# Recurrent block, sparse feed-forward and attention on one core: the last block's norms and sparse inputs on VectorE

## The chip, the cores and the metric

The kernel runs on one core of a Trainium2 chip. A core has a matrix engine (TensorE, PE in the profile), a vector engine (VectorE, DVE), a scalar engine (ScalarE, ACT), a general engine (GpSimd, POOL), and queues for transfers, most of which are issued by SyncE (SP). Each engine takes its own instructions in the order in which they were compiled and waits at semaphores for the others. The metric is the device time of one execution in microseconds (us); the shown time is the median of several runs.

## The reference, cut to what matters

The input is x, 4 x 1024 tokens of 256 features. Four residual layers follow one another, each on the layer-normalized x: a linear recurrent unit, a sparse feed-forward layer, attention with 8 heads, and the sparse feed-forward layer once more. What the change touches is the end of the first and the start of the second:

```python
out = out2[0] - out2[1] + o
y = jax.nn.gelu(out @ w1_w + w1_b, approximate=False)
y = y @ w2_w + w2_b + out
y = (y - mean) * rsqrt(var + LN_EPS) * ln_g + ln_b          # x = x + y
...
xc = jnp.einsum('ngf,gf->ng', x2d.reshape(n, g, 4), conv_w) + conv_b
xn = (xc - mean(xc)) * rsqrt(var(xc) + BN_EPS) * gamma + beta # over all 4096 tokens
logits = gelu(xn) @ lin_w.T + lin_b                          # once for outputs, once for inputs
score_out = softmax(logits)
s_v_out, s_i_out = top_k(score_out, 32)
full = x @ weight              # only its 32 best of 256 outputs are kept, times their scores
in_branch = x_sparse @ weight  # x with only its 32 best of 256 inputs, times their scores
x = x + out_branch + in_branch + bias
```

Two points set the order. The second norm in the sparse layer is a batch norm: its mean and variance are taken over all tokens, so no GELU of that layer can start before the last token's convolution. And the convolution wants the layer norm of the finished x of the last tokens.

## The kernel before

Tokens lie on the 128 partitions, so 4096 tokens are 32 tiles, and four tiles make a block; there are 8 blocks, 0 to 7 (NBLK = 8), and the last is block 7. x stays in SBUF throughout. A scheduler fixes the order of instructions on each engine at compile time; `tc.issue_after(i)` is a demand on it that what follows is issued after instruction i. It is the compiled order that the chip executes.

**Recurrent layer** (`Lru`, up to about 265 us). `outputs` makes out for one block, then GELU, the second product and the residual `ot` (VectorE, L455), turns it back into `py` (TensorE, L465), takes the layer norm of `py` with bn_stats and bn_aggr (`layer_norm`, tiles `ly_*`; the inverse root is a chain of small VectorE steps, L55 to L66, then the shift, minus mean times rstd, L136), and adds y to x. For the last block this is cut in two halves of 256 tokens (`halves`), whose buffers are given as `bufs`. There the normalized `yn` is made by ScalarE (L474) and multiplied by the gain and added to x by VectorE (L479, L480). The base is added to x on GpSimd beforehand.

**Start of the sparse layer** (`Ffn.head`, first called for earlier blocks in between). For a block it takes the layer norm of x (tiles `fx_*`, result `norm_f`), makes `xn` per tile (ScalarE, L145, in `normalized_t`), transposes it (TensorE, L147, into `pt`), copies `pt` to `ft` (ScalarE, L524), writes `ft` to DRAM as `tt` (SP, L527), convolves it (TensorE, L529, into `pc`), adds the bias (ScalarE, L533, `xc`) and takes bn_stats of it (VectorE, L534). `xn` has two buffers. Block 6 goes through `head` as a whole in two pairs of tiles, block 7 as two calls of one pair. So the end of the recurrent layer has four rounds of pt, ft, pc: two for block 6 and two for block 7.

**Batch norm and first tiles.** `norm_scale` makes the scale `bs` and the shift `bt` of the batch norm on VectorE (L542 to L548, with the small steps at L55 to L66). `gelu(0)` and `gelu(1)` (ScalarE, L587) treat the 512 tokens of blocks 0 and 1. `Ffn.tile` makes the logits of a tile `pl` (TensorE, L554 and L556), the first maxima (VectorE, L674), the negated maximum `nm` (GpSimd, L613), the exponentials `ex` (ScalarE, L615), the remaining steps of the top 32 (match_replace and max on VectorE, L674), the reciprocal `rs` (VectorE, L630), the dense product `pf` from `tt` (TensorE, L567), and the two branches (`ob`, `xg`, and the additions to x at L659 and L662). The first eight tiles run so before attention starts; the other 24 run inside the attention phase as side work.

**Weights for later.** `wfs` is the sparse weight in two parts, a rounded high part (ScalarE, L1151) and the remaining low part (GpSimd, L1152); it is first used in the attention phase. `attn_weights` loads the attention weights (SP: `wa` at L712, `wdf` at L715), splits `wdf` in `wd` (L718, L719), squares it (`wds`, GpSimd, L724) and goes on to make products of the attention weights in between the first tiles. On SP stand in this order: the last writes of `ft`, the first `tt` load, the `wa` loads, `wdf`, the second `tt` load.

**Attention and the last layer.** The keys of batch 0 need the finished x of tiles 0 to 7 (layer norm `ax_*`, transposes at L147, products `pml`, then the two parts `kh` and `kl`), and its first scores `sc` follow. Attention runs head by head, 345 to 1285 us, with the other sparse tiles merged in; the last sparse layer follows to the end.

Of the kernel before, what the change touches and what calls it, by code (L numbers as in the profile page):

```python
# [10 lines left out]
F32 = mybir.dt.float32  # L11
# [4 lines left out]
AF = mybir.ActivationFunctionType  # L16
ALU = mybir.AluOpType
# [4 lines left out]
P = 128  # L22
# [6 lines left out]
NBLK = B * T // 512  # L29
# [15 lines left out]
V_BETA = 22  # L45
# [75 lines left out]
    return c, s, last  # L121


def layer_norm(nc, pool, tag, views, rstd=None, shift=None):

    n = len(views)
    mv = pool.tile([P, n, 2], F32, tag=f"{tag}_mv", name=f"{tag}_mv")
    if rstd is None:
        both = pool.tile([P, 2, n], F32, tag=f"{tag}_rs", name=f"{tag}_rs")
        rstd, shift = both[:, 0, :], both[:, 1, :]  # L130
    for i, v in enumerate(views):
        st = pool.tile([P, 6], F32, tag=f"{tag}_st", name=f"{tag}_st", bufs=4)
        nc.vector.bn_stats(st, v)
        nc.vector.bn_aggr(mv[:, i, :], st)
    rsqrt(nc, pool, tag, mv[:, :, 1], rstd)
    nc.vector.scalar_tensor_tensor(shift, mv[:, :, 0], -1.0, rstd, ALU.mult, ALU.mult)  # L136
    return rstd, shift


def normalized_t(nc, pool, psum, tag, ptag, views, rstd, shift, ident):  # L140

    pt = psum.tile([P, KD, len(views) * P], ptag, "pt")
    for i in range(len(views)):
        xn = pool.tile([P, D], F32, tag="fx_xn", name="xn", bufs=2)
        nc.scalar.activation(xn, views[i], AF.Identity, bias=shift[:, i : i + 1], scale=rstd[:, i : i + 1])  # L145
        for k in range(KD):
            nc.tensor.transpose(pt[:, k, i * P : (i + 1) * P], xn[:, k * P : (k + 1) * P], ident)  # L147
    return pt
# [46 lines left out]
class Lru:  # L195
# [226 lines left out]
    def outputs(self, r, xs, xnt, h, pairs, last, tag="po", bufs=None):  # L422

        nc, w, sp, vecs = self.nc, self.w, self.sp, self.vecs
        tiles = range(2 * pairs[0], 2 * pairs[-1] + 2)
        sl = slice(tiles[0] * P, (tiles[-1] + 1) * P)
        n = len(tiles) * P
        ot, zt = bufs or self.buffers()
        for c in range(KD):
            co = slice(c * P, (c + 1) * P)  # L430
            po = self.psum.tile([P, 512], tag, "po")[:, 0:n]
            self.inputs(po, r, 2, c, xnt, sl, stop=False)
            terms = [
                (self.w_mid[r][k][e][:, co], h[k][e][:, sl.start + r : sl.stop + r]) for k in range(KD) for e in range(2)
            ]
            for i, (lt, v) in enumerate(terms):
                nc.tensor.matmul(po, lt, v, start=False, stop=(i == len(terms) - 1))
            nc.scalar.activation(ot[:, c, :], po, AF.Identity, bias=self.ob[:, r, c : c + 1])
            yield
        for c in range(KD):  # L440
            pz = self.psum.tile([P, 512], "pu", "pz")[:, 0:n]
            for k in range(KD):
                nc.tensor.matmul(
                    pz, w[:, k, 2, c * P : (c + 1) * P], ot[:, k, :], start=(k == 0), stop=(k == KD - 1)
                )
            last_gelu = nc.scalar.activation(zt[:, c, :], pz, AF.Gelu, bias=vecs[:, V_B1 + c : V_B1 + c + 1])
        self.last_gelu = last_gelu.ins
        yield
        for c in range(KD):
            pz = self.psum.tile([P, 512], tag, "pz2")[:, 0:n]  # L450
            for k in range(KD):
                nc.tensor.matmul(
                    pz, w[:, k, 3, c * P : (c + 1) * P], zt[:, k, :], start=(k == 0), stop=(k == KD - 1)
                )
            nc.vector.scalar_tensor_tensor(  # L455
                ot[:, c, :], pz, vecs[:, V_B2 + c : V_B2 + c + 1], ot[:, c, :], ALU.add, ALU.add
            )
        yield
        pys = []
        for j in range(len(tiles) // 2):  # L460
            py = self.psum.tile([P, 2, D], "pu" if tag == "pu" else "py", "py")
            for i in range(2):
                tk = slice((2 * j + i) * P, (2 * j + i + 1) * P)
                for k in range(KD):
                    nc.tensor.transpose(py[:, i, k * P : (k + 1) * P], ot[:, k, tk], self.ident)  # L465
            pys += [py[:, 0, :], py[:, 1, :]]
        rstd, shift = layer_norm(nc, sp, f"ly{len(tiles)}", pys)
        gain, base = self.brow[:, 0, :], self.brow[:, 1, :]
        for q, tile_q in enumerate(tiles):
            xt = xs[tile_q]  # L470
            yn = sp.tile([P, D], F32, tag="yn", name="yn", bufs=3)
            if last:
                nc.gpsimd.tensor_tensor(xt, xt, base, ALU.add)
            self.last_yn = nc.scalar.activation(  # L474
                yn, pys[q], AF.Identity, bias=shift[:, q : q + 1], scale=rstd[:, q : q + 1]
            ).ins
            if last:
                engine = nc.vector if bufs else nc.gpsimd
                engine.tensor_tensor(yn, yn, gain, ALU.mult)  # L479
                engine.tensor_tensor(xt, xt, yn, ALU.add)  # L480
            else:
                nc.gpsimd.tensor_tensor(yn, yn, gain, ALU.mult)
                nc.gpsimd.tensor_tensor(yn, yn, base, ALU.add)
                nc.gpsimd.tensor_tensor(xt, xt, yn, ALU.add)
        yield


class Ffn:
# [9 lines left out]
        self.counted = 0  # L498
        self.dram, self.turned, self.full = None, {}, {}

    def head(self, blk, sp, psum, ptag, pairs=(0, 1), xtag="fx", ttag="ft"):


        nc, w = self.nc, self.w
# [3 lines left out]
        norm = self.norm[blk]  # L508
        tiles = slice(2 * pairs[0], 2 * pairs[-1] + 2)
        tokens = slice(256 * pairs[0], 256 * pairs[-1] + 256)  # L510
# [8 lines left out]
        for i, j in enumerate(pairs):  # L519
            r = slice(2 * j, 2 * j + 2)  # L520
            xs = self.x[blk * 4 + 2 * j : blk * 4 + 2 * j + 2]
            pt = normalized_t(nc, sp, psum, xtag, ptag, xs, norm[:, 0, r], norm[:, 1, r], w.ident)
            tt = sp.tile([P, KD, 256], F32, tag=ttag, name="ft", bufs=2 if self.dram else 1)
            nc.scalar.copy(tt, pt)  # L524
            yield
            if self.dram:
                nc.sync.dma_start(self.turned[blk][:, :, j * 256 : (j + 1) * 256], tt)  # L527
            for k in range(KD):
                nc.tensor.matmul(  # L529
                    pc[k * 64 : (k + 1) * 64, i * 256 : (i + 1) * 256], w.cw[:, k, :], tt[:, k, :], start=True, stop=True  # L530
                )
# [6 lines left out]
    def norm_scale(self, sp):  # L538

        nc, w = self.nc, self.w  # L540
        bmv = sp.tile([P, 2], F32, tag="bmv", name="bmv")
        nc.vector.bn_aggr(bmv, self.bst[:, 0 : self.counted, :].rearrange("p a b -> p (a b)"))  # L542
        bs = self.bp.tile([P, 1], F32, tag="bs", name="bs", bufs=2)
        rsqrt(nc, sp, "bn", bmv[:, 1:2], bs)
        nc.vector.tensor_tensor(bs, bs, w.vecs[:, V_GAMMA : V_GAMMA + 1], ALU.mult)
        bt = self.bp.tile([P, 1], F32, tag="bt", name="bt", bufs=2)
        nc.vector.tensor_tensor(bt, bmv[:, 0:1], bs, ALU.mult)
        nc.vector.tensor_tensor(bt, w.vecs[:, V_BETA : V_BETA + 1], bt, ALU.subtract)  # L548
        self.bs, self.bt = bs, bt

    def logits_product(self, dst, i):
        nc, w = self.nc, self.w
# [29 lines left out]
            nc.sync.dma_start(self.full[blk][:, 2 * j : 2 * j + 2, :], v)  # L582
            yield

    def gelu(self, blk):
        x = self.xc[blk]
        return self.nc.scalar.activation(x, x, AF.Gelu, bias=self.bt, scale=self.bs).ins  # L587

    def tile(self, i, sp, psum, tags, out=None, fast=False, parts=None, tt=None, fine=False):
# [395 lines left out]
def run(*gens):  # L985
    for g in gens:
        for _ in g:
            pass
# [58 lines left out]
def tile_kernel(ctx: ExitStack, tc: tile.TileContext, x_in, w_lru, vecs_in, rows, w_ffn, lin_t, w_attn, w_down, out):  # L1047
    nc = tc.nc
# [7 lines left out]
    x = [t[:, q, :] for t in blocks for q in range(4)]  # L1056
# [12 lines left out]
    w = Weights()  # L1069
# [12 lines left out]
    with ExitStack() as c1:  # L1082
# [56 lines left out]
        for i in (0, 1, 0, 1, 0, 1, 1):  # L1139
            next(halves[i])  # L1140
        with tc.issue_after(lru.last_gelu):
            run(f1.head(NBLK - 2, lru.sp, psum, "pt"))
        run(*(f1.head(NBLK - 1, lru.sp, psum, "pu", (i,), "lx", "zt") for i in range(2)))

    with ExitStack() as c2:
        sp = c2.enter_context(tc.tile_pool(name="at_s", bufs=2))
# [2 lines left out]
        wqk, wvo, wd = two([P, KD, HEADS * HD], "wqk"), two([P, PAIRS, D], "wvo"), two([P, KD, P], "wd")  # L1149
        wfs = two([P, KD, D], "wf")  # L1150
        nc.scalar.copy(wfs[0], w.wf)  # L1151
        nc.gpsimd.tensor_tensor(wfs[1], w.wf, wfs[0].bitcast(F32), ALU.subtract)  # L1152
        at = Attention(tc, x, ident, ident64, wqk, wvo, wd, sp, wp)
        with ExitStack() as c4:
            psum = Banks(
# [1 line left out]
            )  # L1157
            fp = c4.enter_context(tc.tile_pool(name="f_t", bufs=4))
            weights = attn_weights(nc, fp, psum, "at", w_attn, w_down, wqk, wvo, wd, at, ident64)
            f1.norm_scale(sp)  # L1160
            tts = [f1.load(blk, fp, f"tt{blk}") for blk in range(2)]
            f1.gelu(0)
            with tc.issue_after(f1.gelu(1)):
                warm(nc, sp, AF.Exp)
            tiles = [
# [174 lines left out]
```

## Time and profile before

| | |
|---|---|
| time, median of 3 runs | 1511.01 us (1509.11 to 1512.66) |
| the profiled execution's own time | 1507.37 us |
| its span in the trace | 1505.6 us |
| busy, TensorE (PE) | 1278.4 us, 85% |
| busy, VectorE (DVE) | 1181.0 us, 78% |
| busy, ScalarE (ACT) | 1018.0 us, 68% |
| busy, GpSimd (POOL) | 683.0 us, 45% |
| mean granted TensorE clock | 0.952 of full speed |
| instructions in the trace | 28728 |

In a row of the timeline the first number is the start in us from the start of the span, the second the time that this group of instructions took; then come the engine, the line of the kernel, the operation, its output and inputs by name, their sizes and types, and how many there are (x2: two such instructions grouped). In square brackets stands how long the engine was idle before it, and what ended that idle time. PEld is the loading of weights into TensorE, SPq a transfer issued by SP. The TensorE clock is the share of full speed that was granted.

### The profile page before, as it was taken

How to read it: one execution, taken by the hardware profiler on the slowest of the kernel's cores; microseconds unless marked ns; L12 is line 12 of the kernel's file. 1: busy time of each engine (PE TensorE's matmuls, PEld its weight loads, DVE VectorE, ACT ScalarE, POOL GpSimd, SP SyncE). 2: the span in 40 equal slices, each digit the busy share in tenths (PEclk: the TensorE clock that was granted, in tenths of full speed). 3: DMA queues.
4: the chain of work that ended last, by engine and by line, in shares of the span. 5: the costliest groups of instructions: out<-in, count | busy, mean ns of one | idle time of the engine just before them, and what ended most of it. 6: DMA issues, size and time to landing. Idle time of an engine off the chain costs nothing. (4 is left out here: it accounts for less than half of the span.)

```text
span 1505.6 us, 28728 instructions
## 1 busy us (share of the span) xinstructions
PE 1278.4 (85%) x10136; PEld 947.3 (63%) x10136; DVE 1181.0 (78%) x3682; ACT 1018.0 (68%) x2152; POOL 683.0 (45%) x849
## 2 busy tenths in 40 slices
PE   4899998887998998898988988889999999576765
PEld 3645555465776777676766766677777877244544
DVE  8988676796778876977777778777676675599998
ACT  5334535666878877787877687877877776566664
POOL 2024523352555454454534543545443534067776
PEclk9999999799999999999999999999999999678898
DMA  3010000432553443353434344433444444000000
GB/s 119 20 55 15 22 21 29 144 105 50 92 88 72 81 86 67 61 89 75 77 73 79 61 69 80 75 74 71 71 85 85 85 85 85 1 15 25 22 25 29
DMA packets 288754, 96.52 MB, mean 64 GB/s; under 512 B 268377, under 2 KB 284770, under 8 KB 288610
## 3 DMA queue, kind: packets, MB, share of 16 engines
q1 hardware_dynamic: 283522, 88.90, 29.6%
q10 hardware_dynamic: 5088, 5.78, 1.1%
q8 instruction: 80, 1.31, 0.4%
q14 instruction: 64, 0.52, 0.1%
HBM read 16.01 MB, written 11.53 MB: 18 GB/s over the span
## 5 line engine op out<-in xcount | busy, mean ns | idle before, releaser
L898 POOL TENSOR_TENSOR pd<-pr,pd 128x1024 f16<-128x1024 f32 x128 | 273.6, 2142 | 259.3 <-ACT pd L897 200.1
L890 DVE TENSOR_REDUCE nm<-sc 128x1 f32<-128x1024 f32 x256 | 308.4, 1217 | 74.8 <-PE sc L886 73.2
L894 ACT ACTIVATE pr<-sc,nm 128x1024 f32<-128x1024 f32 x256 | 286.1, 1120 | 89.8 <-DVE nm L892 54.7
L886 PE MATMUL sc<-kh,qs 128*128 128x512 f32 x512 | 184.4, 438 | 28.5 <-ACT pr L894 21.0
L886 PE MATMUL sc<-kl,qs 128*128 128x512 f32 x512 | 161.7, 396 | 0.0
L674 DVE MATCH_REPLACE8 wk<-m,wk 128x256 f32<-128x256 f32 x384 | 155.3, 408 | 0.1
L910 ACT COPY p<-ptp 128x512 f32<-128x512 f32 x224 | 124.1, 591 | 44.4 <-PE ptp L905 32.5
L674 DVE MAX8 m<-wk 128x8 f32<-128x256 f32 x384 | 150.7, 413 | 0.4
L905 PE MATMUL ptp<-ident,pr 128*128 128x128 f32 x1024 | 139.2, 276 | 13.3 <-ACT pr L894 12.0
L930 PE MATMUL pmo<-p,la 128*64 128x128 f32 x2048 | 140.2, 284 | 5.9 <-ACT ft L524 2.9
L905 PEld LDWEIGHTS ptp<-ident,pr 128*128 128x128 f32 x1024 | 116.2, 141 | 35.5 <-ACT pr L894 21.7
L897 ACT CAST pd<-pr 128x1024 f16<-128x1024 f32 x128 | 133.5, 1054 | 4.6 <-DMA d<-pd 3.6
L930 PEld LDWEIGHTS pmo<-p,la 128*64 128x64 f32 x2048 | 119.6, 142 | 24.7 <-issue 4.7
L886 PEld LDWEIGHTS sc<-kh,qs 128*128 128x128 f32 x512 | 85.2, 195 | 53.9 <-ACT pr L894 32.9
L886 PEld LDWEIGHTS sc<-kl,qs 128*128 128x128 f32 x512 | 96.6, 189 | 23.2 <-issue 1.4
L930 PE MATMUL pmo<-d,lb 128*64 128x128 f16 x3072 | 101.5, 220 | 8.7 <-DVE qs L853 2.6
L930 PEld LDWEIGHTS <-lb 128*64 128x64 f16 x3072 | 90.7, 110 | 26.6 <-issue 19.9
L628 POOL TENSOR_TENSOR ex<-ex,wk 128x512 f32<-128x512 f32 x61 | 77.8, 1276 | 58.4 <-DVE wk L674 48.9
L926 POOL COPY rows<-rs 128x128 f32<-128x128 f32 x128 | 36.3, 297 | 120.4 <-PE pmo L938 71.7
L941 DVE TENSOR_TENSOR on<-pmo,rb 128x128 f32<-128x128 f32 x128 | 36.4, 284 | 64.8 <-ACT rb L940 64.3
L147 PE MATMUL pt<-ident,xn 128*128 128x128 f32 x256 | 48.9, 310 | 44.0 <-ACT xn L145 32.3
L699 PE MATMUL pf<-wf,vt 128*128 128x256 f32 x288 | 80.9, 424 | 3.9 <-ACT vt L697 3.4
(307 smaller groups left out, 2766.1 us busy)
## 6 DMA issues: line engine op xcount, KB each, us to landing
tt<-ft SPq DMA_DIRECT2D x16, 256.0 KB
tt<-tt SPq DMA_DIRECT2D x8, 512.0 KB
out<-x SPq DMA_DIRECT2D x32, 128.0 KB
x<-in_x ACTq DMA_DIRECT2D x6, 512.0 KB
pf<-pfs SPq DMA_DIRECT2D x12, 256.0 KB
full<-pf SPq DMA_DIRECT2D x24, 128.0 KB
d<-pd SPq DMA_TRANSPOSE x128
wa<-in_w_attn SPq DMA_DIRECT2D x2, 640.0 KB
```

The lines of the kernel that those rows point to most:

```text
L147: nc.tensor.transpose(pt[:, k, i * P : (i + 1) * P], xn[:, k * P : (k + 1) * P], ident)
L628: pool.tensor_tensor(ex, ex, wk, ALU.subtract)
L674: ins = make(*args).ins
L699: nc.tensor.matmul(dst, vt[:, k, :], w.wf[:, k, :], start=(k == 0 and bias is None), stop=(k == KD - 1))
L886: nc.tensor.matmul(sc[:, sl], qs[:, j, q * P : (q + 1) * P], kk[:, sl], start=(i == 0), stop=(i == 1))
L890: nc.vector.tensor_reduce(nm, sc, AX.X, ALU.max, negate=True)
L894: nc.scalar.activation(pr, sc, AF.Exp, bias=nm, accum_out=ssum[:, j : j + 1])
L897: nc.scalar.copy(pd[:, 0, :], pr)
L898: nc.gpsimd.tensor_tensor(pd[:, 1, :], pr, pd[:, 0, :], ALU.subtract)
L905: nc.tensor.transpose(pt[:, kk, :], pr[:, kc * P : (kc + 1) * P], self.ident)
L910: nc.scalar.copy(dst, pt)
L930: nc.tensor.matmul(po[j * HD : (j + 1) * HD, 0, :], v, pts[j][:, c, :], start=(n == 0), stop=(n == len(terms) - 1),)
```

## The change

Four edits. First, for the two halves of the last block, `layer_norm` gives back the mean and the shift is left out; `yn` is (py - mean) * gain and x is yn * rstd + x, both one scalar_tensor_tensor on VectorE per tile, so that the ScalarE step and the two VectorE steps of before are replaced. Second, in `head` for blocks 6 and 7 (`fast`), the eight `xn` are made by a tensor_scalar with two pointer scalars on VectorE, no longer by ScalarE. Third, GELU of block 0 is called for its first 128 tokens, and then for the other 384. Fourth, the low part of `wfs` on GpSimd is issued behind the last step of the batch norm's scale and shift.

```diff
@@ layer_norm @@
-def layer_norm(nc, pool, tag, views, rstd=None, shift=None):
+def layer_norm(nc, pool, tag, views, rstd=None, shift=None, mean=False):
...
     rsqrt(nc, pool, tag, mv[:, :, 1], rstd)
+    if mean:
+        return rstd, mv[:, :, 0]
     nc.vector.scalar_tensor_tensor(shift, mv[:, :, 0], -1.0, rstd, ALU.mult, ALU.mult)
     return rstd, shift
@@ normalized_t @@
-        nc.scalar.activation(xn, views[i], AF.Identity, bias=shift[:, i : i + 1], scale=rstd[:, i : i + 1])
+        if fast:
+            nc.vector.tensor_scalar(xn, views[i], rstd[:, i : i + 1], shift[:, i : i + 1], ALU.mult, ALU.add)
+        else:
+            nc.scalar.activation(xn, views[i], AF.Identity, bias=shift[:, i : i + 1], scale=rstd[:, i : i + 1])
@@ Lru.outputs @@
-        rstd, shift = layer_norm(nc, sp, f"ly{len(tiles)}", pys)
+        rstd, shift = layer_norm(nc, sp, f"ly{len(tiles)}", pys, mean=bufs is not None)
...
+            if bufs:
+                mean = shift[:, q : q + 1]
+                nc.vector.scalar_tensor_tensor(yn, pys[q], mean, gain, ALU.subtract, ALU.mult)
+                nc.vector.scalar_tensor_tensor(xt, yn, rstd[:, q : q + 1], xt, ALU.mult, ALU.add)
+                continue
...
             if last:
-                engine = nc.vector if bufs else nc.gpsimd
-                engine.tensor_tensor(yn, yn, gain, ALU.mult)
-                engine.tensor_tensor(xt, xt, yn, ALU.add)
+                nc.gpsimd.tensor_tensor(yn, yn, gain, ALU.mult)
+                nc.gpsimd.tensor_tensor(xt, xt, yn, ALU.add)
@@ Ffn.norm_scale @@
-        nc.vector.tensor_tensor(bt, w.vecs[:, V_BETA : V_BETA + 1], bt, ALU.subtract)
         self.bs, self.bt = bs, bt
+        return nc.vector.tensor_tensor(bt, w.vecs[:, V_BETA : V_BETA + 1], bt, ALU.subtract).ins
@@ Ffn.gelu @@
-    def gelu(self, blk):
-        x = self.xc[blk]
+    def gelu(self, blk, tokens=slice(0, 512)):
+        x = self.xc[blk][:, tokens]
@@ tile_kernel @@
-            run(f1.head(NBLK - 2, lru.sp, psum, "pt"))
-        run(*(f1.head(NBLK - 1, lru.sp, psum, "pu", (i,), "lx", "zt") for i in range(2)))
+            run(f1.head(NBLK - 2, lru.sp, psum, "pt", fast=True))
+        run(*(f1.head(NBLK - 1, lru.sp, psum, "pu", (i,), "lx", "zt", True) for i in range(2)))
...
-        nc.gpsimd.tensor_tensor(wfs[1], w.wf, wfs[0].bitcast(F32), ALU.subtract)
...
-            f1.norm_scale(sp)
+            with tc.issue_after(f1.norm_scale(sp)):
+                nc.gpsimd.tensor_tensor(wfs[1], w.wf, wfs[0].bitcast(F32), ALU.subtract)
             tts = [f1.load(blk, fp, f"tt{blk}") for blk in range(2)]
-            f1.gelu(0)
+            for tokens in (slice(0, P), slice(P, 512)):
+                f1.gelu(0, tokens)
```

In the compiled programs, counted without the parts that the profile adds, the numbers change little: VectorE 3178 instructions instead of 3172, ScalarE 1773 instead of 1784, TensorE, GpSimd and SP as many as before.

## Prediction

> **What bounds the kernel now.** I read the page first. Its shares (PE 85%, DVE 78%) are averages over three phases, and its chain of waits reaches back only to about 1216 us, so the changed stretch (253 to 287 us) has to be read from the timeline, where the idle time before an instruction and its releaser stand in brackets. The first piece shows the last two blocks' normalized rows turned and convolved.
>
> ```profile
> 258.95 1.02 ACT L474 ACTIVATE yn<-py,ly_rs 128x256 f32<-128x256 f32 x2 [5.50 <-DVE norm_f L136]
> ...
> 259.87 1.08 ACT L145 ACTIVATE xn<-x,norm_f 128x256 f32<-128x256 f32 x2
> ...
> 260.51 1.18 PE L147 MATMUL pt<-ident,xn 128*128 128x128 f32 x4 [4.10 <-ACT xn L145]
> ...
> 262.36 0.58 ACT L524 COPY ft<-pt 128x512 f32<-128x512 f32 x1
> ...
> 262.99 1.12 PE L529 MATMUL pc<-ft,cw 128*64 128x256 f32 x4 [1.30 <-ACT ft L524]
> ...
> 270.99 0.59 ACT L524 COPY ft<-pt 128x512 f32<-128x512 f32 x1 [0.56 <-PE pt L147]
> ```
>
> TensorE is empty for 4.10 us, until ScalarE has made xn; then four rounds of pt, ft, pc follow, one behind the other (pc starts at 262.99, 265.83, 268.78, 271.62: 2.9 us a round). ScalarE idles 5.50 us for VectorE's norm. The view by stretches shows who is full, and the granted TensorE clock:
>
> ```profile
> 256.50:260.50 4.00, 0.00 (x0) 0.00 (x0) 3.90 (x34) 1.55 (x4) 0.00 (x0) 1.00 0.02 4
> ...
> 264.00:268.00 4.00, 3.32 (x14) 1.67 (x12) 2.80 (x26) 2.50 (x5) 0.00 (x0) 0.50 0.38 131
> ...
> 274.00:284.00 10.00, 5.76 (x10) 3.02 (x10) 5.66 (x23) 5.02 (x11) 1.55 (x3) 0.50 0.89 308
> ```
>
> Columns: stretch, length, busy us of PE, its weight loads, DVE, ACT, POOL, the clock, the DMA share, GB/s. Before the first transposes **VectorE is the full engine** (3.90 of 4.00); ScalarE has 2.4 us free. The second piece of the timeline shows the batch norm, the loads and the first top-k tiles:
>
> ```profile
> 274.15 0.84 SPq L561 DMA_DIRECT2D tt<-tt  x2
> ...
> 274.94 1.13 DVE L66 SCALAR_TENSOR_TENSOR bs<-bn_t,bs 128x1 f32<-128x1 f32 x1
> ...
> 276.99 0.43 SPq L715 DMA_DIRECT2D wdf<-in_w_down  x1
> ...
> 277.70 1.52 ACT L587 ACTIVATE xc_f<-xc_f,bt,bs 128x512 f32<-128x512 f32 x2 [2.98 <-DVE bt L548]
> ...
> 280.67 0.76 DVE L674 MAX8 m<-pl 128x8 f32<-128x256 f32 x2 [3.01 <-PE pl L556]
> ...
> 284.13 0.61 POOL L724 TENSOR_TENSOR wds<-wdf 128x256 f32<-128x256 f32 x1 [2.41 <-DMA wdf<-in_w_down]
> ...
> 284.72 0.19 POOL L613 TENSOR_SCALAR nm<-m 128x2 f32<-128x2 f32 x1
> ...
> 286.18 0.17 DVE L630 RECIPROCAL rs<-ssum 128x2 f32<-128x2 f32 x1 [1.15 <-ACT ex L615]
> ```
>
> From 286.2 us to about 337 VectorE runs top-k without a pause (43.0 busy of the 45 us from 300 to 345). So what ends at 286.18 is what counts: rs of tile 1. It waits for ex(1), that for nm(1), and nm(1), whose maxima were there at 283.1, stands on GpSimd behind wds, which waits for the load of wdf. That load is behind the tt loads on SP, and these wait for the write of the last ft. **The chain is: last ft, its write, the loads, wds, nm(1), rs(1), VectorE's 50 us.** Batch norm and GELU lie beside it.
>
> **The change part by part.** I use the order of instructions of both compiled programs on each engine; the durations are the trace's.
>
> *The yn on VectorE.* Four ACT yn, four multiplications and four additions (0.42 us each) become eight scalar_tensor_tensor (the 128x256 ones at L455 took 0.475 us). VectorE pays 8 x 0.05 = 0.4 us; four shift steps go (0.3). But three yn now stand ahead of the block-6 norm, two of them between the two additions that complete the second half's ot, so this half's py start 0.8 us later.
>
> *The eight xn on VectorE.* No row is a 128x256 tensor_scalar with two pointer scalars. From below: 0.348 us, the same size with one pointer. From above: 0.348 + 0.13 = 0.48 us (128x1 steps take 0.27 with two pointers at L62, 0.14 with one at L59). I take 0.42; 8 x 0.42 = 3.4 us onto the full engine. [...]
>
> *The first transposes.* Norm of block 6 was done at 258.91. Ahead of it now come three yn (3 x 0.39), two x (0.79), less one shift (0.07): 260.80. Then one yn (0.39), two bn_stats (0.74), a small step and xn (0.42): 262.4. The transposes start 1.9 us later than 260.51. What comes back: ft was held on ScalarE behind yn and xn (262.36 instead of about 261.7), which now are gone, 0.7. So the first pc is **1.2 us later**. The following rounds are bound by pt, ft, pc in a row, not by xn: the fourth pair of xn is ready about 270.5, 0.4 before its transposes. Last ft, its write and xc: +1.2.
>
> *The clock.* The 4.10 us gap becomes about 5 (py end 0.8 later, the transposes 1.9). The trace has full clock up to the gap and 0.50 from 260.6 to 284.5, with a group of four at 1.11 instead of 0.66. [...]
>
> *The low part of wf behind batch norm.* The step of 1.13 us against 0.16 elsewhere lies in the shadow of GpSimd's subtraction (274.80, 1.26 us). Moved, it gives back **0.97 us** of batch norm. The subtraction then waits for bt (277.9) on GpSimd; behind it is nm(0), needed only after 281, so it costs nothing; without that gap, its 1.26 us.
>
> *GELU of 128 tokens.* One call of 512 took 0.80 us; 128 columns about 0.35 (between 0.20 for one column, L155, and 0.47 for 256, L615): 0.45 earlier. Together: the first logits start at 278.56 + 1.2 - 0.97 - 0.45 = 278.3. VectorE's first maxima gain 0.2 us.
>
> *What is late next.* Both gains end at a wait that they don't move. wdf lands at 284.05 + 1.2 = 285.25 (transfers run at 308 GB/s and start with the write). And the order changes: TensorE makes the whole of pf(0) before pl(1), so maxima(1) come at about 284.1 instead of 282.4, and on GpSimd nm(1) now stands behind wds, sc(0) and also wd (0.73 us): it starts 1.55 after the landing instead of 0.67, +0.9. rs(1) comes at 286.18 + 1.2 + 0.9 = 288.3. Against that, one match_replace and small steps of the tile's chain (0.5) are done before it. VectorE's long stretch lags by 1.2 + 0.9 - 0.5 = **1.6 us**.
>
> *The entry to attention.* At 337 to 357 us the work is a chain: x(6) 343.70, x(7) 344.97, kh, kl 346.86, xn(7) 351.82, first scores 356.55. In the new order x(7) stands behind kl on VectorE, so tile 7's norm runs after tile 6's and not beside it. Between 0 (covered by pmq and pv) and 2.5 us (346.86 + 0.69 - 344.97, none covered). I take **1.0**, as ScalarE still held xn(7) 1.2 us behind its norm. Some 60 local swaps of neighbours in attention (PE 824 busy of 920 us) and in the last stage I cost at nothing, with 3 us either way.
>
> *Sum:* 1.6 + 1.0 = +2.6 us. The profiled run took 1507.4 us (span 1505.6), which gives 1510.0; the shown median is 1511.0, so I forecast **1513.6**.
>
> **The rivals.** *A, the forecast:* the chain to wdf's landing is later; 55%. Its own range is 1511.5 to 1516.5.
>
> [...] 27%.
>
> *C, slower by x(7) behind kl:* VectorE takes its queue in order, so tile 7's norm waits for tile 6's whole pml, kh, kl. Its price is the full 2.5 us, and with the match_replace's 0.5 not won back the sum is 1.2 + 0.9 + 2.5 = +4.6, 1515.6; it decides as soon as pf(7) is ready before kl, as it was (x(7) ran at 344.97). Against: pmq and pv fill TensorE meanwhile. 18%.
>
> That the change isn't made as said is excluded: both orders show it.
>
> **How the numbers follow.** What can be told from no change is 0.2%, 3.0 us. With the swaps' 3 us around each: A gives 0.02 faster, 0.24 same, 0.29 slower; B 0.16, 0.10, 0.01; C 0.02, 0.02, 0.14. Sum: 0.20, 0.36, 0.44. The range 1507.0 to 1519.0 leaves out the low part of B and the end of C.
>
> **What would show it.** First pt near 262.4 and PE's gap near 5 us; xn on VectorE 0.35 to 0.48; clock 0.50 through all four rounds; the last ft near 272.2; bs steps all 0.16; first logits 278.3; wds about 285.3; nm(1) behind wd; rs(1) 288.3; first scores about 359. I am wrong if the xn cost 0.2 us, if the clock returns by 270, if rs(1) comes before 286.2, or if attention's 920 us change by more than 3.

## The result, and the profile after

The changed kernel takes 1526.3 us (median of 6 runs, 1523.1 to 1528.6), the kernel before 1511.9 beside it: **ratio 1.0091 (95% interval 1.0071 to 1.0111)**, about 14 us slower, outside the forecast range. The profiled execution took 1525.1 us, its span is 1523.4.

The page after, first part:

```profile
PE 1296.8 (85%) x10136; PEld 960.8 (63%) x10136; DVE 1182.2 (78%) x3688; ACT 1010.0 (66%) x2141; POOL 682.1 (45%) x849
```

As many matmuls as before (10136) keep TensorE busy for 18.4 us longer, a little more than the 17.8 by which the span grew; VectorE got 1.2 us more work. That is no handover; it is the same work done slower. The timeline shows that most of it happens outside the part that was forecast. The lines that answer to those of the prediction (start, duration, engine, line, operation; idle time and releaser in brackets):

```profile
263.52 0.73 DVE L149 TENSOR_SCALAR xn<-x,norm_f 128x256 f32<-128x256 f32 x2
...
264.08 1.08 PE L153 MATMUL pt<-ident,xn 128*128 128x128 f32 x4 [5.19 <-DVE xn L149]
...
265.24 0.59 ACT L535 COPY ft<-pt 128x512 f32<-128x512 f32 x1 [10.10 <-PE pt L153]
...
273.87 0.58 ACT L535 COPY ft<-pt 128x512 f32<-128x512 f32 x1 [0.62 <-PE pt L153]
...
277.68 1.26 POOL L1171 TENSOR_TENSOR wf<-wf,wf 128x512 fp32r<-128x512 f32 x1 [0.18 <-ACT wf L1162]
277.82 1.14 DVE L66 SCALAR_TENSOR_TENSOR bs<-bn_t,bs 128x1 f32<-128x1 f32 x1
...
281.13 2.08 PE L567 MATMUL pl<-lint,xc_f 128*128 128x512 f32 x2 [3.92 <-ACT xc_f L598]
...
286.91 0.61 POOL L735 TENSOR_TENSOR wds<-wdf 128x256 f32<-128x256 f32 x1 [2.62 <-DMA wdf<-in_w_down]
...
287.44 0.77 DVE L685 MAX8 m<-pl 128x8 f32<-128x256 f32 x2 [1.71 <-PE pl L567]
...
287.73 0.72 POOL L730 TENSOR_TENSOR wd<-wdf,wd 128x256 fp32r<-128x256 f32 x1
...
288.42 0.19 POOL L624 TENSOR_SCALAR nm<-m 128x2 f32<-128x2 f32 x1
...
289.66 0.20 ACT L626 ACTIVATION_READ_ACCUMULATOR ex<-pl,nm 128x1 f32 x1
...
290.46 0.16 DVE L641 RECIPROCAL rs<-ssum 128x2 f32<-128x2 f32 x1
...
350.47 0.68 DVE L167 TENSOR_TENSOR kl<-pml,kh 128x512 fp32r<-128x512 f32 x1
351.06 0.41 DVE L673 TENSOR_TENSOR x<-x,pf 128x256 f32<-128x256 f32 x1
```

This trace is 1.68 us late already at 230 us, ahead of all edits (the clock was 0.50 for 3.41 us from 156.6 us, in before it was 1.00 there); take that off each start. Then the first transposes stand at 262.40 (forecast 262.4), the last ft at 272.19 (272.2), wds at 285.23 (285.3), rs(1) at 288.8 (288.3), and x(7) does stand behind kl. But rs(1) bears no bracket: VectorE did not wait for it. Its last pause is the 1.71 us before the maxima of tile 1 (m, at 287.44), which wait for this tile's logits on TensorE; from there it works through to rs(1). The first exponentials of attention are 3.8 us later than before, where the sum had 2.6. By the same reckoning the last ones are 16.7 us later: attention itself grew by 13.

The view by stretches, cut at the same instructions in both (columns: stretch, length, busy us of PE, its weight loads, DVE, ACT and POOL with counts, the TensorE clock, DMA share, GB/s). Before, then after:

```profile
360.30:589.40 229.10, 203.97 (x1994) 160.03 (x1992) 182.94 (x476) 181.00 (x364) 114.72 (x120) 0.99 0.44 80
589.40:1018.90 429.50, 377.66 (x3724) 299.82 (x3726) 330.99 (x873) 330.39 (x655) 200.84 (x199) 0.98 0.40 74
1018.90:1063.70 44.80, 39.42 (x438) 31.43 (x434) 33.25 (x83) 35.24 (x73) 19.95 (x23) 1.00 0.38 72
1063.70:1272.50 208.80, 195.53 (x2111) 158.77 (x2108) 139.87 (x283) 156.37 (x282) 94.35 (x80) 1.00 0.49 86
```

```profile
365.70:601.50 235.80, 209.33 (x1993) 164.73 (x1992) 181.08 (x476) 180.23 (x365) 114.88 (x120) 0.96 0.44 77
601.50:1031.20 429.70, 379.67 (x3699) 300.83 (x3701) 330.72 (x873) 330.00 (x654) 201.27 (x201) 0.97 0.40 74
1031.20:1080.60 49.40, 43.37 (x458) 34.67 (x456) 33.89 (x83) 35.20 (x72) 19.31 (x21) 0.94 0.35 65
1080.60:1290.90 210.30, 197.06 (x2112) 160.25 (x2109) 139.80 (x283) 156.32 (x282) 94.24 (x80) 0.99 0.48 85
```

Attention takes 925.2 us instead of 912.2, and its TensorE busy time goes from 816.6 to 829.4. VectorE, ScalarE and GpSimd are as busy as before. The clock column falls where the time goes: 0.99 to 0.96, 1.00 to 0.94. Part of the 13 us is the pair of traces: the trace of before took 1507.37 us, against a median of 1511.9.

No edit touches attention's code. But the scheduler orders the whole program from times that it assumes, and the edits moved these. To make one compiled order of the other, from attention on at the least 304 of 7694 matmuls have to be moved (the expectations below count them another way, as 331), 379 instructions of VectorE, 139 of ScalarE and 76 of GpSimd. Nearly three quarters of the matmuls among them are in the first batch (to about 600 us), the others in small groups up to the last layer. One of the places, after and before:

```profile
1045.42 0.62 PE L897 MATMUL sc<-kh,qs 128*128 128x512 f32 x2
1045.88 0.62 PE L897 MATMUL sc<-kl,qs 128*128 128x512 f32 x2
...
1050.50 1.09 PE L916 MATMUL ptp<-ident,pr 128*128 128x128 f32 x8
1053.75 0.76 PE L897 MATMUL sc<-kh,qs 128*128 128x512 f32 x2 [2.17 <-DVE qs L864]
...
1055.30 3.14 PE L941 MATMUL pmo<-p,la 128*64 128x128 f32 x32
```

```profile
1034.57 0.73 PE L886 MATMUL sc<-kh,qs 128*128 128x512 f32 x2
1035.14 0.63 PE L886 MATMUL sc<-kl,qs 128*128 128x512 f32 x2
1035.67 1.09 PE L905 MATMUL ptp<-ident,pr 128*128 128x128 f32 x8
1038.37 0.73 PE L886 MATMUL sc<-kh,qs 128*128 128x512 f32 x2 [1.61 <-DVE qs L853]
...
1039.50 1.97 PE L930 MATMUL pmo<-p,la 128*64 128x128 f32 x32
```

Before, four matmuls of scores (sc, from 1034.57) stand right ahead of these transposes (ptp); in the new order they have gone further ahead. The wait for qs behind the transposes grows from 1.61 to 2.17 us, and the 32 matmuls behind it take 3.14 us instead of 1.97. In the traces the clock changes only at steps of 3.41 us (more on this at the end). In the step with the shorter wait TensorE was busy for 0.53 of the time, and the clock stayed at 1.00; in the one with the longer wait it was 0.37, and at 1054.3 the clock fell to a half for 3.4 us.

### The profile page after: what moved, and what is told of

It reads as the page before. It is cut to its first block, busy times and chain, and to the rows that moved or that the text cites. A ratio compares the mean times of both kernels' runs of the same rounds, so it can differ in the third digit from the quotient of the medians.

```text
span 1523.4 us, 28732 instructions
## 1 busy us (share of the span) xinstructions
PE 1296.8 (85%) x10136; PEld 960.8 (63%) x10136; DVE 1182.2 (78%) x3688; ACT 1010.0 (66%) x2141; POOL 682.1 (45%) x849
## 3 DMA queue, kind: packets, MB, share of 16 engines
q8 instruction: 80, 1.31, 0.4%
## 5 line engine op out<-in xcount | busy, mean ns | idle before, releaser
L905 ACT ACTIVATE pr<-sc,nm 128x1024 f32<-128x1024 f32 x256 | 285.8, 1119 | 86.0 <-DVE nm L903 52.9
L153 PE MATMUL pt<-ident,xn 128*128 128x128 f32 x256 | 50.1, 317 | 44.8 <-ACT xn L151 27.7
```

What stands on the lines that cost most here:

```text
L905: nc.scalar.activation(pr, sc, AF.Exp, bias=nm, accum_out=ssum[:, j : j + 1])
```

## Experiments

"In the order of" means: every instruction that the program traces from the attention phase on is tied behind its predecessor in a recorded order, engine by engine. The computation is the same in all runs.

### Edits and order apart: after_ordB, before_ordA, before_ordA0

```diff
+    keep_order(tc, tail_mark)   # at the end of tile_kernel; names below shortened
...
+        order = [mine[k] for k in flat[at + 1 : at + 1 + n]]
+        for first, then in zip(order, order[1:]):
+            tc.add_manual_dep(then, first.name, mybir.DependencyInfo(NoSync, DATA), reason="keep_order")
```

> The changed kernel, with one thing added: every instruction from the attention phase on stands on its engine in the order that it has in the kernel before. Theory 1 (the loss is made by the new order of the attention phase): the head alone is left, its first scores were 3.8 us late once the 1.7 us by which the whole trace starts late are taken off, so about 1515 to 1516, 10 to 12 us under the changed kernel. Theory 2 (the edits themselves cost it, through late weights, late tiles or the clock, whatever the order): about 1526, as the changed kernel.

> The kernel before, none of the four edits, but every instruction from the attention phase on in the order that it has in the changed kernel. Theory 1: lag grew from 5.4 to 18.4 us between the first and the last scores, so 10 to 13 us slower than before, about 1522 to 1525. Theory 2: no change, 1510 to 1513.

> The kernel before with the changed kernel's order in the first batch of attention alone (up to about 600 us), and the order of before behind it. Theory 1, with the loss where the trace shows it: +6.6 us (the lag goes from 5.4 to 12.0 us there), about 1518.5; the other 6 us come from the later pieces. Were the loss spread evenly over the moves: three quarters of them lie in this piece, so about +10. Theory 2: no change.

| head | order of attention | us, median | ratio to before (95%) |
|---|---|---|---|
| after | before | 1517.0 | 1.0033 (1.0021 to 1.0046) |
| before | after | 1520.2 | 1.0046 (1.0027 to 1.0064) |
| before | after in the first batch only | 1516.7 | 1.0021 (1.0007 to 1.0036) |

The order costs 7 us without any edit (4 to 10), the edits 5 us without the order (3 to 7); together 12, of the measured 14 (11 to 17). Theory 2 falls. The ties themselves cost nothing that shows: wfs_real_ordB and nm_first_ordB below, tied to the order of before and with a small edit of their own, take 0.9984 and 0.9996 of its time. But theory 1 had the sizes too high: before_ordA stayed under its forecast of 10 to 13 us and before_ordA0, with 3 us (1 to 5), under its 6.6. I had taken these from one pair of traces, and the trace of before (1507.4 us) was a quick execution of a kernel whose median over 129 runs is 1512.7. Over several traces the two orders lie apart all the same: from the first to the last exponentials, attention takes 912.2 to 920.4 us in the seven traces with the old order and unfilled stalls, 925.2 and 926.2 in the two with the new one. The piece around 1020 us, first in after_ordB, then in before_ordA:

```profile
1031.10:1075.90 44.80, 39.48 (x440) 31.45 (x435) 33.21 (x83) 35.20 (x72) 19.98 (x23) 1.00 0.38 72
```

```profile
1026.90:1076.30 49.40, 43.36 (x457) 34.64 (x457) 33.88 (x83) 35.23 (x73) 19.23 (x21) 0.94 0.35 65
```

44.80 us with the old order and 49.40 with the new one, whichever head runs before it. In the ten traces with the old order in this piece it takes 44.8 to 46.5, in the two with the new one 49.4. The step of 3.41 us with the wait for qs repeats too: busy 0.53 and full clock behind it in after_ordB, 0.36 and half clock in before_ordA.

### Which edit makes the head's loss: only_gelu_ordB, no_gelu_ordB

```diff
# only_gelu_ordB: before, with
-            f1.gelu(0)
+            for tokens in (slice(0, P), slice(P, 512)):
+                f1.gelu(0, tokens)
# no_gelu_ordB: the changed kernel, with
-            for tokens in (slice(0, P), slice(P, 512)):
-                f1.gelu(0, tokens)
+            f1.gelu(0)
```

> The kernel before with one edit alone, GELU of block 0 in 128 and 384 tokens; from the attention phase on the order of before is kept. Theory 1 (what the head loses through this edit is order: pf(0) ahead of pl(1), nm(1) behind wd, x(7) behind kl): the first logits 0.4 us earlier, rs(1) 0.9 us later, the first exponentials of attention 2 to 2.5 us later, time +2. Rival (the edit only makes the first logits earlier, and the head's loss comes from the norms on VectorE): rs(1) and the time within 0.5 us of before.

> The changed kernel without the split of GELU, so the norms and the xn on VectorE alone; from the attention phase on the order of before. Theory 1: last ft +1.2 us, and no more than that behind it, rs(1) and first exponentials +1.2, time +1 to +2. Rival: the head's whole loss, rs(1) +2.6 and the first exponentials +4, time +3 to +5.

1516.4 us, ratio 1.0024 (1.0001 to 1.0047), and 1516.6, ratio 1.0016 (0.9993 to 1.0039). In the traces, each against its own start as above, rs(1) comes 1.31 us later by GELU alone and 1.33 by the norms alone (2.60 in the changed kernel): up to there the two add up, and the GELU split, which was to start the logits sooner, costs as much as the norms, as its new order puts nm(1) behind wd. The last ft moves by 1.20 with the norms and by nothing without them.

At the entry to attention they do not add up. x(7) comes 4.25, 2.60 and 4.42 us later, and the first exponentials 4.6, 3.4 and 3.8: the GELU split alone loses as much as all edits together. Theory 1 missed this in both runs (2 to 2.5 us for GELU, 1.2 for the norms); the rival had 4 for the norms, but 2.6 at rs(1), where 1.33 came. Nor is x(7) behind kl the reason, as theory 1 had it for GELU: in only_gelu_ordB x(7) starts at 349.08 us, ahead of kl at 349.73. What holds the entry there stays open.

The fourth edit has no run of its own, but the trace above shows that it did not do what it was written for. The subtraction is on GpSimd, the last batch norm step (bt) on VectorE, and `issue_after` made no wait between the two: the subtraction starts at 277.68, 2.7 us ahead of bt, and the step beside it still takes 1.14 us. The next section moves it behind an instruction of its own engine.

### The batch norm and the load of wdf: wfs_real_ordB, nm_first_ordB, nm_exp_ordB

```diff
# all three: the low part of wf issued behind nm of tile 0, on its own engine
-        nc.gpsimd.tensor_tensor(wfs[1], w.wf, wfs[0].bitcast(F32), ALU.subtract)
+            with tc.issue_after(f1.last_nm):
+                nc.gpsimd.tensor_tensor(wfs[1], w.wf, wfs[0].bitcast(F32), ALU.subtract)
# nm_first_ordB: GpSimd's work on wdf behind nm of tile 1; nm_exp_ordB: ScalarE's too
+    with tc.issue_after(ffn.last_nm):                                   # nm_first_ordB
+    with tc.issue_after(ffn.last_nm), tc.issue_after(ffn.last_exp):     # nm_exp_ordB
+        halves(wd, t)
```

> The kernel before with the low part of wf really moved: it is issued on GpSimd behind nm(0), so that no batch norm step stands beside it; from the attention phase on the order of before. Theory 1 (the batch norm is hidden behind the load of wdf): the step of 1.13 us becomes 0.16, the first logits come 0.97 us earlier, rs(1) and the time stay (within 0.5 us). Rival (the batch norm is on the path): rs(1) and time 1.0 us less.

> The kernel before with two moves on GpSimd alone: the low part of wf behind nm(0), and wds and wd behind nm(1), so that nm(1) no longer waits for the load of wdf; from the attention phase on the order of before. Theory 1 (the load of wdf, through nm(1), is what starts VectorE's long stretch): rs(1) 2.0 us earlier, and the first exponentials of attention 1.5 to 2 us earlier; time -1.5 to -2, which may lie within the noise of the clock. Rival (another wait ends there): rs(1) within 0.5 us.

> Kernel before with the low part of wf behind nm(0), wds and wd on GpSimd behind nm(1), and the copy of wd on ScalarE behind the exponentials of tile 1, so that neither engine waits for the load of wdf ahead of tile 1's top-k; the order from the attention phase on is left to the scheduler. Theory 1 (the load held rs(1) through two engines): rs(1) 2 us earlier, VectorE's long stretch 1 to 2 us earlier; the time follows the attention order that the scheduler makes, so between -2 and +5. Rival: VectorE waits for wdf next, at the copy of pn, and rs(1) alone moves.

wfs_real_ordB: 1512.1 us, ratio 0.9984 (0.9964 to 1.0004). All three steps at L66 take 0.16 us and the first logits come 0.97 us earlier. But rs(1) came 0.85 us earlier too, where the forecast had less than 0.5: wdf landed sooner in this run (wds at 283.48). Whether the batch norm brought that stays open: wds starts 12.2 to 12.3 us behind the last ft in three of the six traces with this move, 13.1 to 13.6 in the other three, and 13.0 to 13.5 in the eight without it. nm_first_ordB: 1512.4, ratio 0.9996 (0.9974 to 1.0017), and rs(1) only 0.34 us earlier, where the forecast had 2.0. Its timeline:

```profile
282.35 0.19 POOL L613 TENSOR_SCALAR nm<-m 128x2 f32<-128x2 f32 x1 [0.26 <-DVE m L674]
...
284.40 0.40 ACT L718 CAST wd<-wdf 128x256 fp32r<-128x256 f32 x1 [2.12 <-DMA wdf<-in_w_down]
...
284.71 0.47 ACT L615 ACTIVATE ex<-pl,nm 128x256 f32<-128x256 f32 x1
...
285.95 0.17 DVE L630 RECIPROCAL rs<-ssum 128x2 f32<-128x2 f32 x1 [1.81 <-ACT ex L615]
```

nm(1) no longer waits, but ex(1) now stands on ScalarE behind the copy of wd, which waits for the same load. My reading "that for nm(1)" had named one of two queues. With both freed (nm_exp_ordB; the scheduler made the order of before by itself) the load is off the path:

```profile
286.02 0.47 ACT L615 ACTIVATE ex<-pl,nm 128x256 f32<-128x256 f32 x1 [0.30 <-POOL nm L613]
...
287.50 0.16 DVE L630 RECIPROCAL rs<-ssum 128x2 f32<-128x2 f32 x1
287.65 0.61 POOL L724 TENSOR_TENSOR wds<-wdf 128x256 f32<-128x256 f32 x1 [1.67 <-DMA wdf<-in_w_down]
```

This trace is 3.5 us late ahead of these steps, so rs(1) is 2.2 us and the first exponentials of attention 1.9 us earlier than before. The time, 1513.4, ratio 1.0004 (0.9986 to 1.0022), doesn't show it: 1.9 us less still lies within the interval.

### The clock: fill_ordB, nm_exp_fill

```diff
+    extra = [nc.tensor.transpose(pt[:, 0, 0:P], ident, ident).ins for _ in range(fill(ptag))]
...
+                nc.tensor.matmul(pc[0:64, i * 256 : i * 256 + P], w.cw[:, 0, :], w.ident, start=True, stop=True).ins
+                for _ in range(fill(ptag))
```

> The kernel before with its own order from the attention phase on, and 98 extra matmuls of TensorE in front of eight stalls of 1.2 to 2.1 us that the trace of before shows in attention (transposes or products of the identity, into places that the next instruction overwrites). Nothing else changes, and each filler is shorter than its stall. Theory 1 (attention loses time where a window of 3.4 us has TensorE busy for less than about 0.45 of it and the next ones run at half clock): of some 24 to 40 us at half clock in attention 15 to 20 go, and each saves 0.25 to 0.4 us: 4 to 8 us faster than before, about 1505 to 1509. Rival (the half clock goes along with the loss but doesn't make it, or the fillers only take the place of the stalls): within 2 us of before, or slower by up to 10 us if all the fillers add to the path.

> The three moves of the run above, the attention order of before, and the 98 fillers. Theory 1: rs(1) 2 us earlier, first exponentials of attention 1 to 2 us earlier, and the fillers' 4 to 8 us: 5 to 9 us faster than before, about 1504 to 1508. Rival: no faster than before.

1524.2 us, ratio 1.0083 (1.0055 to 1.0110), and 1520.3, ratio 1.0053 (1.0028 to 1.0078). A miss, and fill_ordB's timeline says why:

```profile
699.66 0.66 PE L159 MATMUL pt<-ident,xn 128*128 128x128 f32 x4
702.17 4.83 PE L544 MATMUL pc<-ident,cw 128*64 128x128 f32 x27 [1.85 <-DVE qs L875]
```

The stall is still there, 1.85 us, and the fillers (`pc<-ident,cw`) come behind it: they write into the same PSUM buffer as the product that they stand ahead of, and had to wait for VectorE's qs step to give it free. In a row of 27 they take 4.83 us here, more than the stall that they were to fill; the 3.41 us with the stall stay 0.43 busy, and the clock falls at 702.6. So the fillers were added to the path. The time at half clock fell a little (mean of the runs 159 and 149 us, against 162 for before beside them) and the time rose, so the test doesn't show what the clock costs. That stays open.

What can be said rests on the runs' own clocks. In the traces the clock is 1.00 or 0.50, so the time at half clock is 2 x (1 - mean clock) x time. Over 129 runs of the kernel before, on four chips but always the same program, the time goes with it at a correlation of 0.82 and 0.27 us a us (0.17 to 0.35 on each chip by itself): 25 runs at a clock of 0.949 or more have a median of 1509.1 us, 28 at 0.943 or less 1516.3. The mean time at half clock is 164 us for before, 170 for after_ordB, 181 for before_ordA, 194 for the changed kernel. By that slope some 8 of the 14 us, an estimate, go with the 30 us more at half clock (5 to 10 by the slopes of single chips). The traces put these 30 us in attention: 24 to 43 us at half clock there in the seven traces with the old order and unfilled stalls, 55 and 58 in the two with the new one, and 81 to 86 behind attention in all nine. This is a tie and no proof: a longer stall costs time itself (2.17 us against 1.61 at the wait for qs above), and 3.41 us at half clock came with it there.

### Two more orders: nm_exp_yn, nm_exp_xn

The head of nm_exp_ordB, with the orders that the scheduler makes for the yn alone and for the xn alone (`keep_order` as above).

> The head of nm_exp_ordB, whose first exponentials come 1.9 us earlier, with a third order from the attention phase on: the one that the scheduler makes when the norms on VectorE alone are edited (49 matmuls moved against before, not 331). Theory 1 (an order costs what it makes of stalls and half clock, whatever edit it comes from; few moves, small change): within 4 us of before, half clock near that of before. Rival (every order but the old one is worse): 5 us slower or more.

> The same head with a fourth order, the one that the scheduler makes when the xn on VectorE alone are edited (84 matmuls moved). Theory 1: within 5 us of before, and the time of both runs follows the half clock of their own records at about 0.26 us a us. Rival: 5 us slower or more, or no tie to the clock.

1510.5 us, ratio 0.9990 (0.9977 to 1.0003), and **1510.1, ratio 0.9982 (0.9969 to 0.9995)**, with 167 and 155 us at half clock. The rival falls: an order is not worse for being new. Within each run's own executions the time follows the half clock at 0.17 and 0.24 us a us. The second is faster than before, by 2.7 us (1 to 5), of which its own trace shows 1.1 at the first exponentials of attention; with one order it is no rule.

## Why the prediction was wrong

- **The step that failed:** "Some 60 local swaps of neighbours in attention ... and in the last stage I cost at nothing, with 3 us either way." No line stood behind the nothing or the 3 us. There are at the least 304 moves on TensorE alone, and the new order costs 7 us (4 to 10) with no edit at all.
- **The head, too small.** The sum had 2.6 us; with the order of before kept, the edits cost 5 (3 to 7), and the first exponentials of attention are 3.8 us late in the trace.
- **Right up to the load of wdf.** The xn cost 0.41 us (0.73 for two; forecast 0.42), yn from PSUM 0.48; first transposes, last ft and wds within 0.1 us; no clock back in the four rounds. The 27% of B counted on full clock from the third round on; no run shows that; the clock was 0.50 from 260.8 to 284.7 us before and from 262.4 to 286.3 after.
- **The last wait, wrong.** By the forecast chain (wds, nm(1), ex(1)) rs(1) could have started at 288.2 us, as the sums of tile 1 were there: the 288.3 of the forecast. It came at 288.8, since VectorE was not ready. VectorE had started on m(1) at 285.8 and not at the forecast 284.1, and had no pause from there on. So "batch norm and GELU lie beside it" does not hold for the changed kernel: they lead to the first logits (279.5, forecast 278.3), these through pf(0) to the logits of tile 1, and these to m(1). The 0.5 us credited for "one match_replace and small steps" fell away with it, as there was no idle time left for them to fill. The entry took 1.2 more (forecast 1.0).
- **"That the change isn't made as said is excluded: both orders show it"** was false for the low part of wf. I read a wait into a call that made none across engines. The 0.97 us, booked as hidden, were not quite hidden: by the numbers above rs(1) could have come some 0.6 us earlier, an estimate.
- **Rival C**, the slower one, named x(7) behind kl, and that stands in the trace, but it was inside the head's 3.8 us and not what decided.
- "Attention's 920 us change by more than 3" was named as what would make me wrong. It did.

## What to carry to other kernels

Where a scheduler orders the whole program, an edit in one stage can move instructions in every later stage. Compare the compiled orders to the end, and hold the order of the untouched part fixed before judging an edit of a few us. Note the mean clock of each run beside its time. And when the named releaser of a wait is removed, look on every engine between for a second instruction that waits for the same thing.

## What the runs showed of the hardware

All stretches at half clock last a multiple of 3.41 us (3.41 to 23.89 us in the traces of before and after; but for the last of a run, which its end cuts), on a grid that doesn't move within a run. A window here is one step of this grid. The clock fell also behind windows in which TensorE was busy for part of the time. I counted the windows of all fourteen traces by the share in which TensorE was busy. At full clock and busy 0.3 to 0.4, all 73 were followed by half clock; at 0.4 to 0.5, 58 of 115; at 0.5 to 0.6, 31 of 274; at 0.6 to 0.7, 19 of 315; above, 12 of 4503. At half clock and busy under 0.7, all 228 stayed there; at 0.7 to 0.8, 67 of 70; at 0.8 to 0.9, 49 of 69; at 0.9 and more, 18 of 299. The stall of 2.17 us at 1051.6 stood in a window that was busy for 0.37, and half clock followed at 1054.3. The four rounds stayed at 0.50 with TensorE busy for 3.32 of 4.00 us before (264 to 268) and 3.22 of 4.00 after (267 to 271). Where the grid lies against the stalls may be why the same program took 1506.5 to 1523.4 us; no run here sets it, so that isn't shown. Nor do these counts say what sets the clock.
